# Block transposes and copies for every quad of an attention kernel, two placed tiles, output weights loaded one at a time, queries loaded by quad

## The chip, the cores and the metric

The kernel runs on one core of one Trainium2 chip. The metric is the device time in microseconds of one execution; the median of several runs counts. Engines are named as the profile names them: PE is TensorE, DVE is VectorE, ACT is ScalarE, POOL is GpSimd, SP is SyncE, which here only issues transfers.

## The reference, cut to what matters

Four conditional layers are added onto x (32 sequences of 32 rows, 512 wide). The first three are projections with weights picked by index; the fourth is attention over a paged cache, where nearly all of the time goes.

```python
B, S, HID, D, HQ, HK = 32, 32, 512, 128, 32, 8      # as drawn here; 16 pages of 32 keys
q = rope(rmsnorm(x @ Wq.T)); k = rope(rmsnorm(x @ Wk.T)); v = x @ Wv.T
k_all = concatenate([k_cache[block_table], k]); v_all = concatenate([v_cache[block_table], v])
scores = einsum('bqhd,bkhd->bhqk', q, k_all) * SCALE      # 512 cached keys + 32 new ones
scores = where(valid, scores, -1e30)
probs  = softmax(scores)
o      = einsum('bhqk,bkhd->bqhd', probs, v_all)
x      = x + o.reshape(b, s, HQ * D) @ Wo.T
```

Four query heads share one key head, so that one key head of one sequence is a product of 128 query rows (4 heads x 32 rows) with 544 keys.

## The kernel before, in words

**First part.** x goes through the three small layers tile by tile (8 tiles of 128 rows). Then twelve chunks of 512 columns are projected (`projected`, L296): eight of queries, two of keys, two of values. PE does four accumulating matmuls per tile and chunk; DVE, ACT and POOL normalize and rotate; DVE transposes blocks of 32x32 (L349), and SP stores the heads to HBM (L358), four stores of 64 KB per tile. The weights of the next chunk are loaded on ACT's queue. The output weights `wo` (8 MB) are loaded on SP's queue, four transfers of 512 KB at the start of each of the chunks 3 to 6 (L640). Four tiles of the last chunk are left for later (`FILLS`).

**Attention.** The work is 256 units (b, g), b the sequence and g the key head, and four units of one sequence make a quad. The order on PE, DVE, ACT, POOL and SP is the program's own order, written out by hand: a loop over steps n emits, for each step,

- on SP at g = 0: the keys of the next sequence, 16 pages of 128 KB, behind the new values (`vn`), new keys and queries. On POOL at g = 7: the values, 16 pages. Both live in two homes by turns (`homes[b % 2]`). All of SP's transfers share eight completion slots: one waits until the eighth before it has landed;
- `scores`: two score matmuls (L680, L681) into the only score buffer in PSUM, then one DVE instruction that scales, masks and takes the minimum (L687, `pr`, `low`);
- `exponentials`: ACT's exponential with the sum (L698), and a small copy of the 32 new keys' probabilities into `pq` (L701);
- the probabilities' transpose[...]. For the second quad of a sequence PE transposes four blocks of 128x128 (`flip`, L741) and ACT copies them out (L743). For the first quad DVE transposes blocks of 32x32 (`turn`, L714) and sixteen copies of 32 partitions set the blocks in place (`place`, L730 on ACT, L732 on DVE);
- `values`: four value matmuls (L763) of the unit seven steps back; at a quad's end four more with the new keys' values (L775), and `keep` on DVE (L786, L788, L791), which divides by the sum and transposes;
- `flip_new` once a quad: PE transposes `pq` (L750), ACT copies it out (L752);
- `share`: output matmuls (L808) of the tile of four sequences finished before, dealt over 32 steps. At the first of them the residual x is loaded into a buffer of its own (L807); behind the last, DVE adds (L817) and SP stores (L818).

The places around the change that a sentence can't give:

```python
            if 2 <= n < N + 2 and (n - 2) % QUAD == QUAD - 1:
                flip_new(units[n - 2][0], units[n - 2][1] // QUAD)   # behind values(n)
...
    SHARE = [1, 2] * 5 + [1] + [1, 1, 1, 0] * 5 + [1]
```

Of the kernel before, what the change touches and what calls it, by code (L numbers as in the profile page):

```python
# [19 lines left out]
P = 128  # L20
# [36 lines left out]
def cond_resid_kernel(  # L57
# [44 lines left out]
    pk = const.tile([1, B + B * NPP], I32, name="pk")  # L102
# [5 lines left out]
    nc.sync.dma_start(out=pk, in_=pick)  # L108
# [12 lines left out]
    key_f = const.tile([P, LT], F32, name="key_f")  # L121
# [6 lines left out]
    def constant_values():  # L128
        nc.gpsimd.memset(eps_t, EPS)
        nc.gpsimd.memset(half_pi, HALF_PI)  # L130

        nc.gpsimd.iota(
            key_f[:, :L],
            pattern=[[1, L]],
            base=0,
            channel_multiplier=0,
            allow_small_or_imprecise_dtypes=True,
        )
        nc.vector.memset(key_f[:, L:], -4.0e9)
        nc.vector.tensor_copy(len_f, ii[:, C_SEQ : C_SEQ + B])  # L140
# [18 lines left out]

    class Picked:  # L160
# [3 lines left out]
        def __init__(self, eng, src: bass.AP, at: int, dsts, shape: str):  # L164
            self.eng, self.src, self.at, self.dsts, self.shape = eng, src, at, dsts, shape
            self.rows = []
            for _ in range(AHEAD):
                self.name_next()

        def name_next(self):  # L170
            n = self.at + len(self.rows)
            self.rows.append(
                nc.values_load(
                    pk[0:1, n : n + 1],
                    engines=(self.eng.engine,),
                    min_val=0,
                    max_val=self.src.shape[0] - 1,
                    skip_runtime_bounds_check_because="rows are drawn from the array's own range",
                )
            )  # L180
# [9 lines left out]
    homes, kts, vts, vns, news = {}, {}, {}, {}, {}  # L190
# [4 lines left out]
    def load_keys(b: int):  # L195

        pool = homes[b % 2]
        kt = pool.tile([P, NPP + 1, HK * PSIZE], F32, tag="kt", name=f"kt_{b}")
        qt = pool.tile([P, HQ * S], F32, tag="qt", name=f"qt_{b}")
        kts[b], news[b] = kt, qt  # L200
# [3 lines left out]
    def see_keys(b: int):  # L204

        nc.vector.tensor_scalar(
            mask, key_f, len_f[:, b : b + 1], -1.0e30, ALU.is_ge, ALU.mult
        )

    def load_new_keys(b: int):  # L210
        nc.sync.dma_start(out=kts[b][:, NPP, :], in_=k_d[b])
        nc.sync.dma_start(out=news[b], in_=q_d[b])
# [414 lines left out]
    vnp = ctx.enter_context(tc.tile_pool(name="b_vn", bufs=3, side="right"))  # L627
# [3 lines left out]
    for c in range(1, NCH):  # L631
        if c + 1 < NCH:
            load_qkv(c + 1, nc.scalar)
        if c == 2:
            load_pages(0)
            load_values(0)
        if 3 <= c < 7:
            r = c - 3
            for k in range(D // S):
                nc.sync.dma_start(  # L640
                    out=wo[r * S : (r + 1) * S].rearrange("d (g k) o -> d g k o", g=HK)[:, :, k, :],
                    in_=w_o4[r, k],
                )
        if c == (HQ + HK) // REP:

            while ready:
                store_heads(*ready.pop(0))
            turn.close()
            turn_n.close()
            ps_p = ctx.enter_context(tc.tile_pool(name="b_p", bufs=1, space=PSUM, side="right"))  # L650
            load_new_keys(0)
            open_home(1)
            load_keys(1)
            load_new_keys(1)
            load_pages(1)
            load_values(1)
        for t in range(1 if c == 1 else 0, NT if c < NCH - 1 else NT - FILL):
            projected(c, t, 2)
            if c == NCH - 1 and t == 2:
                load_new_values(0)  # L660
                load_new_values(1)
# [6 lines left out]
    dens, news_p, prs, pos = {}, {}, {}, {}  # L668
# [5 lines left out]
    def scores(b: int, g: int):  # L674
        kt, qt = kts[b], news[b]
# [3 lines left out]
        q = qt[:, g * REP * S : (g + 1) * REP * S]  # L679
# [4 lines left out]
        pr = tp.tile([P, LT], F32, tag="pr", name=f"pr_{b}_{g}", bufs=4)  # L684
# [7 lines left out]
    def exponentials(b: int, g: int, pr, low):  # L692
        quad, u = quad_of(b, g), g % QUAD
        if u == 0:
            dens[quad] = tp.tile([P, QUAD], F32, tag="den", name=f"den_{b}_{g}", bufs=4)
            prs[quad] = {}
            news_p[quad] = tp.tile([P, QUAD, S], F32, tag="pq", name=f"pq_{b}_{g}")
# [3 lines left out]
        nc.scalar.copy(news_p[quad][:, u, :], pr[:, L:])  # L701
        prs[quad][u] = pr
# [3 lines left out]
    turned, placed = {}, {}  # L706

    def turn(b: int, us):
        if 0 in us:
            turned[b] = tp.tile(  # L710
                [P, P // S, QUAD, L // P, S], F32, tag="turned", name=f"turned_{b}", bufs=1
            )
        for u in us:
            nc.vector.transpose(  # L714
                turned[b][:, :, u, :, :].rearrange("p j c s -> p c j s"),
                prs[b, 0].pop(u)[:, :L].rearrange("p (c j s) -> p c j s", j=P // S, s=S),
            )

    def place(b: int, i: int, on_act: int):

        if i == 0:
            placed[b] = tp.tile(
                [P, QUAD, L // P, P], F32, tag="placed", name=f"placed_{b}", bufs=1
            )
        for j in range(P // S):
            dst = placed[b][j * S : (j + 1) * S, :, :, i * S : (i + 1) * S]
            src = turned[b][i * S : (i + 1) * S, j, :, :, :]
            dst, src = (a.rearrange("p u c s -> p (u c) s") for a in (dst, src))
            if j < on_act:
# [3 lines left out]

    pts = {}

    def flip(b: int, g: int):

        pr = prs[quad_of(b, g)].pop(g % QUAD)
        pp = ps_p.tile([P, L // P, P], F32, tag="p", name=f"p_ps_{b}_{g}")
        for c in range(L // P):  # L740
            nc.tensor.transpose(pp[:, c, :], pr[:, c * P : (c + 1) * P], ident)  # L741
        pts[b, g] = tp.tile([P, L // P, P], F32, tag="pt", name=f"pt_{b}_{g}")
        nc.scalar.copy(pts[b, g], pp)  # L743
# [3 lines left out]
    def flip_new(b: int, q: int):  # L747

        pnp = ps_p.tile([P, P], F32, tag="p", name=f"pn_ps_{b}_{q}")
        nc.tensor.transpose(pnp, news_p.pop((b, q)).rearrange("p u s -> p (u s)"), ident)  # L750
        pns[b, q] = tp.tile([P, P], F32, tag="pn", name=f"pn_{b}_{q}", bufs=3)
        nc.scalar.copy(pns[b, q], pnp)  # L752

    def values(b: int, g: int):
# [6 lines left out]
        pt = pts.pop((b, g)) if q else placed[b][:, u, :, :]  # L761
# [8 lines left out]
        if u == QUAD - 1:  # L770
            pn = pns.pop((b, q))

            for i in range(QUAD):
                r = slice(i * S, (i + 1) * S)
                nc.tensor.matmul(po[:, i, :P], pn[r, :], vn[r, q, :], start=False, stop=True)  # L775
            keep(b, q)
# [19 lines left out]
    pfs, x3s = {}, {}  # L796

    BLOCKS = list(range(HALF, HQ)) + list(range(HALF))

    def finish(t: int, ns):  # L800

        for n in ns:
            h = BLOCKS[n]
            if n == 0:
                pfs[t] = ps_p.tile([P, HID], F32, tag="f", name=f"f_ps_{t}")
                x3s[t] = tp.tile([P, HID], F32, tag="x3", name=f"x3_{t}", bufs=1)
# [5 lines left out]
                start=(n == 0),  # L812
                stop=(n == HQ - 1),
            )
            if n == HQ - 1:
# [3 lines left out]

    SHARE = [1, 2] * 5 + [1] + [1, 1, 1, 0] * 5 + [1]

    def share(n: int):
        t, i = divmod(n - 3 - BT * HK, BT * HK)
# [6 lines left out]
    LAG = 7  # L833

    ON_ACT = [[2, 2, 2, 4], [1, 1, 1, 3]]

    FILLS = {0: NT - 4, 1: NT - 3, 3: NT - 2, 5: NT - 1}
# [7 lines left out]
    with tc.manual_schedule(engines=order):  # L845
        for n in range(N + LAG):
            b, g = divmod(n, HK)
            at = B + (b + 1) * NPP
# [4 lines left out]
            if n < N:  # L853
                if g == 0 and 1 <= b < B - 1:
                    load_keys(b + 1)
                    keys = Picked(nc.sync, k_cache, at, page_keys(b + 1), K_SHAPE)
                    load_new_values(b + 1)
                    load_new_keys(b + 1)
                    keys.transfer()
                if g == 7 and 1 <= b < B - 1:  # L860
                    values_in = Picked(nc.gpsimd, v_pages, at, page_values(b + 1), V_SHAPE)
                    values_in.transfer()
                scored = scores(b, g)

            if 2 <= n < N + 2 and units[n - 2][1] >= QUAD:
                flip(*units[n - 2])
            if n < N:
# [4 lines left out]
            if n < N and g in (3, 4):  # L872
                turn(b, (0, 1) if g == 3 else (2, 3))
            if n >= LAG and (n - LAG) % HK < QUAD:
                bm, i = divmod(n - LAG, HK)
                place(bm, i, ON_ACT[bm + 1 >= BT][i])
            if n >= LAG:
                bv, i = divmod(n - LAG, HK)
                values(bv, (i + QUAD) % HK)
                if i == HK - 1:  # L880
                    placed.pop(bv), turned.pop(bv)
            if 2 <= n < N + 2 and (n - 2) % QUAD == QUAD - 1:
                flip_new(units[n - 2][0], units[n - 2][1] // QUAD)
            if n < N and g == HK - 1 and b < B - 1:
                see_keys(b + 1)
            share(n)
            if n >= N + 3:
                finish(NT - 1, range(3 * (n - N - 3), 3 * (n - N - 2)))
        assert not dens and not news_p and not pos and not pts and not pns
        finish(NT - 1, range(12, HQ))  # L890


# [74 lines left out]
```

## Time and profile before

| | us |
|---|---|
| median of 3 runs (1298.12 to 1298.87) | 1298.71 |
| the profiled execution's own time | 1300.91 |
| its span, first to last instruction | 1299.2 |
| PE busy | 1247.2 |
| DVE busy | 762.2 |
| ACT busy | 661.9 |
| POOL busy | 382.0 |

The profiled execution lies 2.2 us above the median; 1.7 us of its time are outside the span. In the page, a group's row gives line, engine, operation, output and input tiles, shapes and count, then busy time and mean length, then the engine's idle time just before, with what ended it. The chain follows the last instruction back to what released it, step by step. The granted clock is the share of full speed at which PE was allowed to run. The first part ends at some 447 us, where the loop over steps begins; the last score matmul is at 1254 us.

### The profile page before, as it was taken

What the parts mean: (1) busy time and instruction counts of PE and PEld (TensorE: products, weight loads), DVE (VectorE), ACT (ScalarE), POOL (GpSimd) and SP (SyncE); (2) the same over time, 40 slices, a digit from 0 to 9 for tenths busy, and PEclk for the clock granted to TensorE, in tenths of its full rate; (3) what the DMA queues carried; (4) which work ended last, traced back from release to release, by engine and by line L of the source; (5) the groups of instructions that cost most, each with busy time, mean ns of one, the idle gap of its engine ahead of it and who ended that gap; (6) DMA issues with size and microseconds to landing.
All of it is one profiled execution on the core that took longest, in us unless ns stands there. A gap on an engine that the chain in (4) does not pass through costs nothing.

```text
span 1299.2 us, 22028 instructions
## 1 busy us (share of the span) xinstructions
PE 1247.2 (96%) x5992; PEld 799.5 (62%) x5992; DVE 762.2 (59%) x1742; ACT 661.9 (51%) x1701; POOL 382.0 (29%) x619
## 2 busy tenths in 40 slices
PE   9999998899999988899999999999999999999998
PEld 5444443334444457767777777777777777777774
DVE  3233775666786046656666666666666665665660
ACT  1232554554455266755555556555655654665550
POOL 2311532223343202422332332233223322432310
PEclk9999999998899999999999999999999999999999
DMA  8985856666445836996888887988877997897710
GB/s 340 421 327 186 247 151 149 152 157 156 111 123 154 252 122 163 218 223 175 209 206 192 199 225 180 202 208 199 219 192 184 219 217 170 214 213 202 175 53 17
DMA packets 181964, 250.80 MB, mean 193 GB/s; under 512 B 26545, under 2 KB 145713, under 8 KB 176082
## 3 DMA queue, kind: packets, MB, share of 16 engines
q1 hardware_dynamic: 152738, 165.35, 47.0%
q0 software_dynamic: 25360, 69.37, 22.8%
q10 hardware_dynamic: 3744, 14.68, 3.2%
q8 instruction: 49, 0.80, 0.3%
q14 instruction: 73, 0.60, 0.2%
HBM read 219.94 MB, written 29.36 MB: 192 GB/s over the span
## 4 chain that ended last, share of the span: by engine, by line
PE 82%; ACT 10%; DMA 3%; DVE 3%; issue 2%; SPq 1%; POOL 0%; DVEq 0%; ACTq 0%
PE qkv L296 26%; PE f_ps L808 16%; PE o_ps L763 15%; PE s_ps L680 8%; PE s_ps L681 7%; ACT placed L730 4%; PE p_ps L741 4%; ACT pr L698 3%; PE adapt L484 2%; DMA wa<-in_w_adapt_dram 2%; DVE pr L687 1%; PE o_ps L775 1%; PE base L464 1%; ACT pq L701 1%; ACT pt L743 0%
## 5 line engine op out<-in xcount | busy, mean ns | idle before, releaser
L185 POOL DMA_DIRECT2D vt<-in_v_cache_dram x480 | 244.8, 510 | 553.1 <-PE o_ps L763 361.9
L296 PE MATMUL qkv<-wq,x3t 128*128 128x512 f32 x768 | 343.2, 608 | 14.5 <-DVE rs L334 14.5
L687 DVE CUSTOM_DVE_ANT_0 pr<-s_ps,mask 128x544 f32<-128x544 f32 x256 | 185.1, 723 | 275.2 <-PE s_ps L681 240.4
L698 ACT ACTIVATE pr<-pr,low 128x544 f32<-128x544 f32 x256 | 191.8, 749 | 167.4 <-DVE low L687 164.1
L296 PEld LDWEIGHTS qkv<-wq,x3t 128*128 128x128 f32 x768 | 148.8, 195 | 204.5 <-issue 204.3
L808 PE MATMUL f_ps<-wo,ot 128*128 128x512 f32 x512 | 257.6, 605 | 0.0
L340 POOL TENSOR_TENSOR ra<-ra,rs 128x512 f32<-128x512 f32 x80 | 101.5, 1269 | 253.3 <-DVE rs L334 194.8
L680 PE MATMUL s_ps<-kt,qt 128*128 128x288 f32 x512 | 170.4, 415 | 1.9 <-DVE low L687 1.9
L763 PE MATMUL o_ps<-vt,placed 128*128 128x128 f32 x1024 | 139.7, 280 | 20.3 <-ACT placed L730 20.3
L342 ACT ACTIVATE ra<-ra,rinv 128x128 f32<-128x128 f32 x320 | 102.2, 390 | 108.0 <-POOL ra L340 106.6
L743 ACT COPY pt<-p_ps 128x512 f32<-128x512 f32 x128 | 75.0, 586 | 159.9 <-PE p_ps L741 159.6
L763 PEld LDWEIGHTS o_ps<-vt,placed 128*128 128x128 f32 x1024 | 131.1, 194 | 36.9 <-ACT placed L730 32.1
L681 PE MATMUL s_ps<-kt,qt 128*128 128x256 f32 x512 | 153.0, 381 | 0.0
L680 PEld LDWEIGHTS s_ps<-kt,qt 128*128 128x128 f32 x512 | 92.7, 191 | 96.5 <-issue 79.4
L732 DVE COPY placed<-turned 32x512 f32<-32x512 f32 x308 | 132.2, 429 | 6.3
L763 PE MATMUL o_ps<-vt,pt 128*128 128x128 f32 x1024 | 135.1, 275 | 0.0
L763 PEld LDWEIGHTS o_ps<-vt,pt 128*128 128x128 f32 x1024 | 126.8, 192 | 1.6
L730 ACT COPY placed<-turned 32x512 f32<-32x512 f32 x204 | 125.5, 615 | 2.0
L681 PEld LDWEIGHTS s_ps<-kt,qt 128*128 128x128 f32 x512 | 97.8, 191 | 27.5 <-DMA vn<-v_d 0.3
L808 PEld LDWEIGHTS f_ps<-wo,ot 128*128 128x128 f32 x512 | 82.2, 190 | 37.2 <-issue 30.1
L318 DVE TENSOR_REDUCE ss<-sq 128x4 f32<-128x512 f32 x80 | 53.8, 673 | 65.5 <-ACT sq L316 65.3
L714 DVE STREAM_TRANSPOSE turned<-pr 128x512 f32<-128x512 f32 x128 | 83.2, 688 | 3.0 <-ACT placed L730 3.0
(95 smaller groups left out, 999.9 us busy)
## 6 DMA issues: line engine op xcount, KB each, us to landing
vt<-in_v_cache_dram POOLq DMA_DIRECT2D x512, 128.0 KB, 6.6
kt<-in_k_cache_dram SPq DMA_DIRECT2D x512, 128.0 KB, 7.1
wa<-in_w_adapt_dram SPq DMA_DIRECT2D x32, 1024.0 KB, 9.4
q_d<-st SPq DMA_DIRECT2D x256, 64.0 KB, 1.8
qt<-q_d SPq DMA_DIRECT2D x32, 512.0 KB, 5.7
wq<-in_w_qkv_dram ACTq DMA_DIRECT2D x10, 1024.0 KB, 5.1
wo<-in_w_o_dram SPq DMA_DIRECT2D x16, 512.0 KB, 8.7
k_d<-st SPq DMA_DIRECT2D x64, 64.0 KB, 1.8
```

The lines of the kernel that those rows point to most:

```text
L185: self.eng.dma_start(out=out, in_=row)
L296: nc.tensor.matmul(ps, x3[:, k, :], w[:, k, :], start=(k == 0), stop=(k == KC - 1),)
L340: nc.gpsimd.tensor_tensor(a, a, s, ALU.add)
L342: nc.scalar.activation(a[:, h, :], a[:, h, :], AF.Copy, scale=rinv[:, h : h + 1])
L680: nc.tensor.matmul(ps[:, first:L], q, kt4[:, :N_LOW, g, :], start=True, stop=True)
L681: nc.tensor.matmul(ps[:, L : first + LT], q, kt4[:, N_LOW:, g, :], start=True, stop=True)
L687: nc.vector.tensor_tensor_reduce(pr, ps[:, first : first + LT], mask, -SCALE, 3.0e38, ALU.add, ALU.min, low)
L698: nc.scalar.activation(pr, pr, AF.Exp, bias=low, scale=-1.0, accum_out=dens[quad][:, u : u + 1])
L730: nc.scalar.copy(dst, src)
L732: nc.vector.tensor_copy(dst, src)
L763: nc.tensor.matmul(po[:, u, :P], pt[:, c, :], vt[:, c, g * D : (g + 1) * D], start=(c == 0), stop=False,)
L808: nc.tensor.matmul(pfs[t], ots[t, h // HALF][:, h % HALF, :], wo[:, h, :], start=(n == 0), stop=(n == HQ - 1),)
```

## The change

- Both quads of each sequence go over DVE's block transposes and the placing copies; PE's `flip` and ACT's copy of it are gone. `place` now takes one quarter j of the keys of all four units per step: one DVE transpose of 128x512 into `turned` (two buffers), then four copies, of which `ON_ACT[j]` on ACT. `placed` has two buffers.
- `pr` holds a quad's four units in one tile (two buffers), and `pq` is filled by one copy of 128x128, inside `flip_new`, which is now emitted in the second step of the next quad, ahead of `place`, `share` and `values`.
- Values are eight steps behind the scores (`LAG` 8). `share` stands ahead of `values`, begins at step 36 and follows another pattern; heads are taken in their natural order.
- The residual x is loaded at the third last output matmul, into the buffer of `os`.
- Queries are loaded by quad (256 KB, three buffers); a sequence's new values at its own g = 0 (two buffers); cached values at g = 0 of their own sequence; the page numbers as small tables of 16.
- `wo` is loaded one transfer after every second tile of the chunks 3 to 6.
- The key numbers for the mask are 16-bit integers.

```diff
+    def load_table(b: int):
+        pages_of[b] = const.tile([1, NPP], I32, tag="pages", name=f"pages_{b}", bufs=4)
+        at = B + b * NPP
+        nc.sync.dma_start(out=pages_of[b], in_=pick[:, at : at + NPP])
...
-        nc.sync.dma_start(out=news[b], in_=q_d[b])
+    def load_queries(b: int, q: int):
+        qts[b, q] = qp.tile([P, HALF * S], F32, tag="qt", name=f"qt_{b}_{q}")
+        nc.sync.dma_start(
+            out=qts[b, q], in_=q_d[b][:, q * HALF * S : (q + 1) * HALF * S]
+        )
...
-        if 3 <= c < 7:
-            r = c - 3
-            for k in range(D // S):
-                nc.sync.dma_start(
...
         for t in range(1 if c == 1 else 0, NT if c < NCH - 1 else NT - FILL):
             projected(c, t, 2)
+            if 3 <= c < 3 + REP and t % 2 == 1:
+                r, k = c - 3, t // 2
+                nc.sync.dma_start(
...
-        pr = tp.tile([P, LT], F32, tag="pr", name=f"pr_{b}_{g}", bufs=4)
+        if u == 0:
+            prs[quad_of(b, g)] = tp.tile([P, QUAD, LT], F32, tag="pr", name=f"pr_{b}_{g}")
+        pr = prs[quad_of(b, g)][:, u, :]
...
-        nc.scalar.copy(news_p[quad][:, u, :], pr[:, L:])
...
+    def place(b: int, q: int, j: int, on_act: int):
+        if j == 0:
+            placed[b, q] = tp.tile([P, QUAD, L // P, P], F32, tag="placed", name=f"placed_{b}_{q}")
+        pr = prs[b, q][:, :, :L].rearrange("p u (c j s) -> p j u c s", j=P // S, s=S)[:, j]
+        part = tp.tile([P, QUAD, L // P, S], F32, tag="turned", name=f"turned_{b}_{q}_{j}")
+        nc.vector.transpose(part, pr)
+        for i in range(P // S):
+            dst = placed[b, q][j * S : (j + 1) * S, :, :, i * S : (i + 1) * S]
+            src = part[i * S : (i + 1) * S]
             dst, src = (a.rearrange("p u c s -> p (u c) s") for a in (dst, src))
-            if j < on_act:
+            if i < on_act:
                 nc.scalar.copy(dst, src)
             else:
                 nc.vector.tensor_copy(dst, src)
-    def flip(b: int, g: int):
-        pr = prs[quad_of(b, g)].pop(g % QUAD)
-        pp = ps_p.tile([P, L // P, P], F32, tag="p", name=f"p_ps_{b}_{g}")
-        for c in range(L // P):
-            nc.tensor.transpose(pp[:, c, :], pr[:, c * P : (c + 1) * P], ident)
...
     def flip_new(b: int, q: int):
         pnp = ps_p.tile([P, P], F32, tag="p", name=f"pn_ps_{b}_{q}")
-        nc.tensor.transpose(pnp, news_p.pop((b, q)).rearrange("p u s -> p (u s)"), ident)
-        pns[b, q] = tp.tile([P, P], F32, tag="pn", name=f"pn_{b}_{q}", bufs=3)
+        pq = tp.tile([P, QUAD, S], F32, tag="pq", name=f"pq_{b}_{q}", bufs=1)
+        nc.scalar.copy(pq, prs[b, q][:, :, L:])
+        nc.tensor.transpose(pnp, pq.rearrange("p u s -> p (u s)"), ident)
+        pns[b, q] = tp.tile([P, P], F32, tag="pn", name=f"pn_{b}_{q}")
         nc.scalar.copy(pns[b, q], pnp)
...
-                x3s[t] = tp.tile([P, HID], F32, tag="x3", name=f"x3_{t}", bufs=1)
+            if h == LATE:
+                x3s[t] = tp.tile([P, HID], F32, tag="os", name=f"x3_{t}", bufs=1)
                 nc.sync.dma_start(out=x3s[t], in_=x_d[t])
...
-    SHARE = [1, 2] * 5 + [1] + [1, 1, 1, 0] * 5 + [1]
+    LAG = 8
+    SHARE = [1, 2, 1, 2] * 2 + [1, 2, 1] + [1, 1, 0, 1] * 4 + [1, 1, 2]
+    BEGIN = BT * HK + LAG - QUAD
...
-    ON_ACT = [[2, 2, 2, 4], [1, 1, 1, 3]]
+    ON_ACT = [3, 3, 3, 2]
-    FILLS = {0: NT - 4, 1: NT - 3, 3: NT - 2, 5: NT - 1}
+    FILLS = {0: NT - 4, 2: NT - 3, 4: NT - 2, 6: NT - 1}
...
             if n < N:
+                if g == 0 and b >= 1:
+                    load_new_values(b)
                 if g == 0 and 1 <= b < B - 1:
                     load_keys(b + 1)
-                    keys = Picked(nc.sync, k_cache, at, page_keys(b + 1), K_SHAPE)
-                    load_new_values(b + 1)
+                    keys = Picked(nc.sync, k_cache, pages_of[b + 1], page_keys(b + 1), K_SHAPE)
                     load_new_keys(b + 1)
+                    load_queries(b + 1, 0)
                     keys.transfer()
-                if g == 7 and 1 <= b < B - 1:
...
+                    if b + 2 < B:
+                        load_table(b + 2)
+                if g == 0 and b >= 2:
+                    values_in = Picked(
+                        nc.gpsimd, v_pages, pages_of.pop(b), page_values(b), V_SHAPE
+                    )
                     values_in.transfer()
+                if g == QUAD and b < B - 1:
+                    load_queries(b + 1, 1)
                 scored = scores(b, g)
                 exponentials(*scored)
             if n in FILLS:
                 projected(NCH - 1, FILLS[n], 2)
...
+            if QUAD <= n < N + QUAD:
+                bq, i = divmod(n - QUAD, HK)
+                q, j = divmod(i, QUAD)
+                if j == 1:
+                    flip_new(bq, q)
+                place(bq, q, j, ON_ACT[j])
+            share(n)
             if n >= LAG:
...
+                values(*units[n - LAG])
...
-            if 2 <= n < N + 2 and (n - 2) % QUAD == QUAD - 1:
-                flip_new(units[n - 2][0], units[n - 2][1] // QUAD)
...
-            share(n)
```

## The prediction

> **What bounds the kernel now.** I read the page's head first, then the chain, the groups by shape, and the timeline of single steps.
>
> ```profile
> span 1299.2 us, 22028 instructions
> PE 1247.2 (96%) x5992; PEld 799.5 (62%) x5992; DVE 762.2 (59%) x1742; ACT 661.9 (51%) x1701; POOL 382.0 (29%) x619
> ...
> PE 82%; ACT 10%; DMA 3%; DVE 3%; issue 2%; SPq 1%; POOL 0%; DVEq 0%; ACTq 0%
> ```
>
> PE is 96% busy and holds 82% of the chain that ended last: a microsecond in which PE waits is lost, and PE work removed is gained. The groups by shape give the work concerned:
>
> ```profile
> L730 ACT COPY placed<-turned 32x512 f32<-32x512 f32 x204 | 125.5, 615 | 2.0
> L741 PE MATMUL p_ps<-ident,pr 128*128 128x128 f32 x512 | 77.8, 275 | 2.1 <-ACT pn L752 0.3
> L743 ACT COPY pt<-p_ps 128x512 f32<-128x512 f32 x128 | 75.0, 586 | 159.9 <-PE p_ps L741 159.6
> L750 PE MATMUL pn_ps<-ident,pq 128*128 128x128 f32 x64 | 17.7, 276 | 2.7 <-ACT pt L743 2.7
> ```
>
> The last row matters most: the 64 transposes of the new keys wait 2.7 us in all, because their input was copied steps earlier. One step's latency stands in the timeline (start, length):
>
> ```profile
> 657.90 0.59 PE L681 MATMUL s_ps<-kt,qt 128*128 128x256 f32 x2
> ...
> 658.54 0.72 DVE L687 CUSTOM_DVE_ANT_0 pr<-s_ps,mask 128x544 f32<-128x544 f32 x1 [1.39 <-PE s_ps L681]
> ...
> 659.31 0.75 ACT L698 ACTIVATE pr<-pr,low 128x544 f32<-128x544 f32 x1 [2.25 <-DVE low L687]
> ...
> 660.18 0.22 ACT L701 COPY pq<-pr 128x32 f32<-128x32 f32 x1
> ```
>
> PE's next work began at 658.34. ACT's first instruction behind the exponential starts 1.84 us later.
>
> [...] (PE idles 20.3 us before o_ps L763 for ACT's copies though score matmuls stand behind). [...] (stretch, PE busy, then PEclk third from the end):
>
> ```profile
> 484.00:485.00 1.00, 0.14 (x1) 0.14 (x2) 0.16 (x1) 0.96 (x3) 0.00 (x0) 1.00 0.87 227
> 485.00:486.00 1.00, 1.00 (x9) 1.00 (x10) 1.00 (x2) 0.89 (x3) 0.00 (x0) 1.00 0.14 43
> 505.00:507.00 2.00, 0.24 (x2) 0.00 (x0) 1.26 (x3) 1.97 (x4) 0.84 (x2) 1.00 1.05 210
> 507.00:508.00 1.00, 0.75 (x4) 0.76 (x5) 0.77 (x2) 0.97 (x3) 0.00 (x0) 0.68 1.08 235
> 508.00:509.00 1.00, 1.00 (x6) 1.00 (x6) 0.53 (x1) 0.28 (x2) 0.00 (x0) 0.50 1.11 234
> ```
>
> Three idle times of 2.00 us (until 484.86, 507.25, 531.29): two are followed by some 3.5 us at 0.5, one by none. The four of 3.63 us (until 226.2, 259.3, 293.5, 327.6) all are; the one of 1.50 (553.5) isn't. [...]
>
> **Part 1: transposes leave PE.** 128 groups of four at 0.44 us (598.10 minus 597.66 in the chain) are 56 us. PE's waits for `placed` change too, some 5 us per 32 steps: the work sums to 97 (per step scores 0.92, values 0.89, new keys 0.11, flips 0.22, new-key flip 0.03, output 0.86, each the distance between starts in the timeline), and 102 elapse (the output blocks in the chain recur from 557.34 to 659.39).
>
> **Part 2: DVE and ACT take them.** DVE: 128 more block transposes at 0.65 us, and 320 copies for 308. ACT: 704 copies for 204; 128 evacuations and 256 small copies go. Per quad (four steps) ACT needs four exponentials at 0.87 (with the accumulator read), 11 copies at 0.62, one pq (128x128; never seen: 0.22 as 128x32 here, 0.39 as L342's; I take 0.30) and pn 0.26: 10.9 us. DVE needs 4 x 0.80 + 4 x 0.65 + 5 x 0.43 + 1.57 for keep + 0.25 = 9.8. A quad had 12.1 (24.2 us per eight steps, 616.95 to 641.14), so neither engine is the bound by sum.
>
> **Part 3: the new wait.** `flip_new` moves to the second step of a quad, straight behind that step's scores on PE. Its pq copy stands on ACT behind the exponential of the *same* scores. PE in order holds values, output and the next scores behind it. Followed from the end of scores of the fourth step (t=0), three outputs per quad:
> - PE: output 0.86, values and new keys to 2.18, scores of the next quad's first step to 3.10.
> - DVE: minimum, transpose, two copies to 2.43; keep's product waits for PE, 2.6 to 3.3; transpose to 3.95; only then the next minimum, low ready at 4.7.
> - ACT: exponential 4.72 to 5.59, three copies to 7.46. PE ends the second step's scores at 5.77.
> - ACT: second exponential to 8.33, pq to 8.63; PE flips at 8.70. PE waited **2.9 us** (2.2 were ACT free).
> - Then values, scores, output, values, scores: 13.3; the mask (0.50 us, one quad in two, behind keep) makes it 13.5.
>
> So 13.5 for 12.1 with three outputs; the same walk gives 15.8 with six (before 13.4: SP's vn loads at 641.14 and 694.69, four quads) and 12.7 with none (before 12.0: 71.8 us from 471.89 to 543.73 for six quads).
>
> **Half clock.** Two of three at 2.0 us and four of four at 3.6 were throttled. I take 0.8 of the 2.9 us waits, each costing half of 3.5 us: 1.4 us per quad, an estimate between 0 and 2.9 (phases of 5.8 us, as from 259.3 to 265).
>
> **Part 4: x loaded late, in os's buffer.** The load is issued three outputs before the end (step 64+32t), on SP behind that step's vn, the register reads, 16 key pages and the table. SP's line before:
>
> ```profile
> 668.14 2.47 SPq L241 DMA_DIRECT2D vn<-v_d  x4
> 670.71 0.52 SPq L211 DMA_DIRECT2D kt<-k_d  x1
> 671.28 0.43 SPq L212 DMA_DIRECT2D qt<-q_d  x1
> 671.90 18.05 SPq L185 DMA_DIRECT2D kt<-in_k_cache_dram  x16
> ```
>
> From the end of step 63's scores: vn (two buffers now) waits for values of step 63, 2.2; vn 2.5; eight register reads at 0.27, 2.1; kt, qt 1.1; the keys 11 to 18 (four batches before took 15.8, 11.0, 15.0, 18.1); x lands 2.7 later at 22 to 29, say 25. DVE's add stands in step 65, before step 66's minimum, and with it every later one. It was due at 11; PE runs out of work at 14 (scores of step 67 need that minimum) and goes on at 26.4. That is 13 us (range 8 to 20), at six tiles; the seventh has no keys ahead. out's store must then land before keep writes os: 3 us, two steps off, hidden; if not, some 1 us.
>
> **Part 5: output weights singly.** The four 3.63 us gaps fall in the chunks with bursts of four, none in the later ones (119.78 us unbroken from 327.62). From 226.21 to 327.62 are 101.4 us for 192 passes at 0.429: 19.0 lost, with the first gap 22.7. Between two single loads there are eight 64 KB stores. I take -20, ends 0 and -23.
>
> **At nothing:** page tables (30 loads of 64 B on SP) and queries by quad (same bytes) lie beside PE work; without that cover 0.3 us of SP each. Keys reach the chip some 4 us later and need to be there 27 us later; only a faster kernel than I forecast would wait. Values (POOL, one step later) need 18 of 27. Integer mask: 32 x 0.50, plus or minus 0.2 each, 6 us.
>
> **Sum** against the profiled execution (1300.9 us, span 1299.2; the median is 2.2 lower). Per 32 steps, with the outputs dealt six, six, five and then three a quad: 15.8+15.8+15.0+5x13.5 = 114, with half clock 125.3, before 102.
> - First eight steps +3; next 24: 6 x 14.1 = 85 for 71.8, +13.
> - Steps 32 to 64: 125 for 100, +25.
> - Six tiles: 125.3 + 13 - 102, +36.3 each, +218.
> - Tail (last copies uncovered, 11 x 0.62 against four values) +5; front -20.
>
> 1300.9 + 244 = 1545, against the median **1543**.
>
> **The rivals.**
> - *No half clock* (2.9 us stay below the throttle as one 2.00 did): 1543 - 62 x 1.4 = **1456**.
> - *Longer throttle or later x*: 5.8 us phases add 0.8 x 1.15 x 62 = 57, 20 us waits 42: some **1595**.
> - *x lands in time* (keys in 11 us, as 620.84 to 631.85, and less beside them): minus 6 x 13, **1465**.
> - *Faster*: the flip's wait hides. PE then needs 89.8 per cycle (97 less the flips), which ACT's 10.9 in quads of three outputs and keep stretch to some 95.5: 0.8 us gained per quad, and 0.3 from the front. So a wait above 1.1 us per quad decides for slower whatever x does. Without it and with x in time, 6.5 x 7 + 3 + 20 are gained: **1230**. For it: the flips wait 2.7 us in all now. Against it: minimum and exponential alone take 1.84. That the transposes don't leave PE is excluded by the changed program's instruction order, which also shows the flip directly behind its step's scores.
>
> **How the numbers follow.** Forecast 0.62, no half clock 0.18, longer 0.10, x in time 0.05, faster 0.04, a tie 0.01. Both slower rivals and the unknown sizes set 1440 to 1620, leaving some 0.18 out. About 0.2% is what a measurement of this kernel tells from no change: faster 0.04, within 0.01, slower 0.95.
>
> **What would show it.** pn_ps should be waiting for ACT pq, some 180 us in 64 times; PEclk near 0.9 from step 8 on; DVE's add waiting for DMA x some 6 times; no gaps from 226 to 330; PE's busy share down to some 80 to 85%. If pn_ps waits less than 40 us in all, the core of this is wrong.

## The result and the profile after

The changed kernel takes 1599.1 us (median of 4 runs, 1590.67 to 1606.81), the kernel before 1298.41 (1295.04 to 1298.87). The ratio is 1.2321, 95% interval 1.224 to 1.2403: slower, with 1543 us forecast. The profiled execution took 1590.67 us, the lowest of the four.

The head of the page after, and its chain:

```profile
span 1589.0 us, 21379 instructions
PE 1279.9 (81%) x5480; PEld 789.2 (50%) x5480; DVE 846.8 (53%) x1882; ACT 867.0 (55%) x1881; POOL 380.2 (24%) x619
...
PE 29%; DVE 8%; ACT 7%; SPq 3%; DMA 3%; issue 2%; ACTq 0%; DVEq 0%
```

PE runs 512 instructions less and is nevertheless busy 33 us longer (1247.2 before): its clock was granted at 0.924, before at 0.987. It also stands still for 309 us, before for 52. DVE and ACT do more, as planned, but neither is near full: the loss lies in waiting. The groups by shape (busy time and mean length, then idle time before them) answer to those shown of the kernel before:

```profile
L733 ACT COPY placed<-turned 32x512 f32<-32x512 f32 x704 | 432.7, 615 | 13.2 <-DVE turned L727 4.2 <-ACT vs L318 0.8
...
L744 PE MATMUL pn_ps<-ident,pq 128*128 128x128 f32 x64 | 23.2, 362 | 155.3 <-ACT pq L743 152.1 <-issue 3.1
...
L743 ACT COPY pq<-pr 128x128 f32<-128x128 f32 x64 | 18.1, 282 | 0.0
...
L811 DVE TENSOR_TENSOR x<-x,f_ps 128x512 f32<-128x512 f32 x8 | 5.5, 688 | 122.8 <-DMA x<-x_d 100.0 <-PE f_ps L802 22.8
```

The 64 small transposes, which waited 2.7 us in all, now wait 155.3. The waits of PE (total us, times, longest) name two more places. The last row is the kernel before's row for the third of them:

```profile
PE pn_ps L744 <- ACT pq L743: 152.1, 63, 2.6
PE s_ps L696 <- DVE low L705: 85.2, 32, 13.5
PE qkv L308 <- DVE rs L346: 36.4, 10, 3.6
...
PE qkv L296 <- DVE rs L334: 14.5, 4, 3.6
```

**The first**, in the timeline of one quad (start, length):

```profile
780.06 0.59 PE L697 MATMUL s_ps<-kt,qt 128*128 128x256 f32 x2
...
780.70 0.72 DVE L705 CUSTOM_DVE_ANT_0 pr<-s_ps,mask 128x544 f32<-128x544 f32 x1 [0.20 <-PE s_ps L697]
...
782.14 0.75 ACT L714 ACTIVATE pr<-pr,low 128x544 f32<-128x544 f32 x1
...
782.89 0.28 ACT L743 COPY pq<-pr 128x128 f32<-128x128 f32 x1
...
783.23 0.33 PE L744 MATMUL pn_ps<-ident,pq 128*128 128x128 f32 x1 [2.57 <-ACT pq L743]
```

The copy's data were ready a step before, but it stands behind the exponential of the newest scores, and PE's transpose stands directly behind those scores. That exponential itself comes some 0.7 us late: its `low` was there at 781.42, but ACT was busy until 782.12 with three placing copies of the step before.

**The second** is the end of an output tile. First the transfers that SP issues (SPq), then DVE and PE:

```profile
730.93 2.62 SPq L253 DMA_DIRECT2D vn<-v_d  x4
736.54 0.34 SPq L217 DMA_DIRECT2D kt<-k_d  x1
736.94 0.42 SPq L222 DMA_DIRECT2D qt<-q_d  x1
737.58 13.61 SPq L192 DMA_DIRECT2D kt<-in_k_cache_dram  x16
751.30 0.29 SPq L165 DMA_DIRECT2D pages<-in_pick_dram  x1
751.68 0.34 SPq L801 DMA_DIRECT2D x<-x_d  x1
```

```profile
754.63 0.69 DVE L811 TENSOR_TENSOR x<-x,f_ps 128x512 f32<-128x512 f32 x1 [17.57 <-DMA x<-x_d]
...
756.02 1.33 PE L696 MATMUL s_ps<-kt,qt 128*128 128x288 f32 x2 [13.49 <-DVE low L705]
```

PE's row names DVE's `low`, but DVE itself was held by the load of x. **The third** is in the first part, PE alone:

```profile
253.72 8.80 PE L308 MATMUL qkv<-wq,x3t 128*128 128x512 f32 x16 [3.64 <-DVE rs L346]
266.15 9.88 PE L308 MATMUL qkv<-wq,x3t 128*128 128x512 f32 x16 [3.64 <-DVE rs L346]
279.67 9.95 PE L308 MATMUL qkv<-wq,x3t 128*128 128x512 f32 x16 [3.63 <-DVE rs L346]
292.39 8.71 PE L308 MATMUL qkv<-wq,x3t 128*128 128x512 f32 x16 [2.77 <-issue]
```

There are 13 such gaps up to 407.12, one at every second tile, where the kernel before had four of 3.63 us. (Ten of the 13 are in the row of waits above; the profile gives the other three as "issue".) The first score matmul starts at 498.2 us, before at 447.2. For this part a gain was forecast.

By place, the spans differ by 289.8 us: 53.1 until the new keys' load of step 8 (525.03, before 471.89), 39.6 from there to that of step 64 (736.54, before 643.81), and 197.1 behind it. The steps were timed on profiled runs; the medians differ by 11 us more.

### The profile page after: what moved, and what is told of

It reads as the page before. It is cut to its first block, busy times and chain, and to the rows that moved or that the text cites. A ratio compares the mean times of both kernels' runs of the same rounds, so it can differ in the third digit from the quotient of the medians.

```text
span 1589.0 us, 21379 instructions
## 1 busy us (share of the span) xinstructions
PE 1279.9 (81%) x5480; PEld 789.2 (50%) x5480; DVE 846.8 (53%) x1882; ACT 867.0 (55%) x1881; POOL 380.2 (24%) x619
## 4 chain that ended last, share of the span: by engine, by line
PE 29%; DVE 8%; ACT 7%; SPq 3%; DMA 3%; issue 2%; ACTq 0%; DVEq 0%
PE f_ps L802 10%; PE o_ps L757 9%; PE s_ps L696 4%; PE s_ps L697 4%; ACT pr L714 3%; ACT placed L733 3%; DVE pr L705 3%; DMA kt<-in_k_cache_dram 2%; DVE ot L786 1%; DVE os L783 1%; SPq L180 1%; PE o_ps L769 1%; DVE turned L727 1%; SPq L192 1%; PE pn_ps L744 1%
## 5 line engine op out<-in xcount | busy, mean ns | idle before, releaser
L733 ACT COPY placed<-turned 32x512 f32<-32x512 f32 x704 | 432.7, 615 | 13.2 <-DVE turned L727 4.2
L308 PE MATMUL qkv<-wq,x3t 128*128 128x512 f32 x768 | 364.0, 635 | 44.7 <-DVE rs L346 36.4
L757 PEld LDWEIGHTS o_ps<-vt,placed 128*128 128x128 f32 x2048 | 287.8, 205 | 112.1 <-issue 95.0
L757 PE MATMUL o_ps<-vt,placed 128*128 128x128 f32 x2048 | 289.7, 288 | 11.2 <-ACT placed L733 11.0
L802 PE MATMUL f_ps<-wo,ot 128*128 128x512 f32 x512 | 267.3, 628 | 3.5 <-DVE ot L786 3.5
L696 PE MATMUL s_ps<-kt,qt 128*128 128x288 f32 x512 | 191.5, 458 | 85.2 <-DVE low L705 85.2
L727 DVE STREAM_TRANSPOSE turned<-pr 128x512 f32<-128x512 f32 x256 | 180.9, 706 | 0.1
L354 ACT ACTIVATE ra<-ra,rinv 128x128 f32<-128x128 f32 x320 | 102.2, 390 | 124.1 <-POOL ra L352 122.9
L744 PE MATMUL pn_ps<-ident,pq 128*128 128x128 f32 x64 | 23.2, 362 | 155.3 <-ACT pq L743 152.1
L802 PEld LDWEIGHTS f_ps<-wo,ot 128*128 128x128 f32 x512 | 101.0, 204 | 52.0 <-issue 37.0
L328 ACT ACTIVATE sq<-qkv 128x512 f32<-128x512 f32 x80 | 46.8, 587 | 81.7 <-PE qkv L308 81.6
```

The lines of the kernel that those rows point to most:

```text
L308: nc.tensor.matmul(ps, x3[:, k, :], w[:, k, :], start=(k == 0), stop=(k == KC - 1),)
L354: nc.scalar.activation(a[:, h, :], a[:, h, :], AF.Copy, scale=rinv[:, h : h + 1])
L696: nc.tensor.matmul(ps[:, first:L], q, kt4[:, :N_LOW, g, :], start=True, stop=True)
L727: nc.vector.transpose(part, pr)
L733: nc.scalar.copy(dst, src)
L757: nc.tensor.matmul(po[:, u, :P], pt[:, c, :], vt[:, c, g * D : (g + 1) * D], start=(c == 0), stop=False,)
```

## The experiments

**1. The wait in front of the transpose.** Theory: it is made by the place of copy and transpose, and costs half-rate time besides. Rivals: the clock doesn't follow, or the wait moves on.

```diff
-                if j == 1:
-                    flip_new(bq, q)
                 place(bq, q, j, ON_ACT[j])
+                if j == 0:
+                    copy_new(bq, q)             # the pq copy, taken out of flip_new
             share(n)
             if n >= LAG:
                 values(*units[n - LAG])
+            if QUAD <= n < N + QUAD and j == 1:
+                flip_new(bq, q)
```

> The changed kernel, with the copy of the new keys' probabilities issued one step earlier on ACT (at the end of the quad's next step) and the transpose issued on PE behind the step's values instead of right behind its scores. Theory (the transpose waits for the copy, and each wait also costs half-rate matmuls behind it): the 152 us of PE idle in front of the transpose go, and 64 x 1.4 us of half rate with them, so 1599 - 240 = about 1360 us, and the granted clock rises above 0.96. Rival 1 (only the wait counts, the clock does not follow from it): 1599 - 152 = about 1447 us with the clock near 0.92. Rival 2 (the wait moves on to the next scores, since ACT is late there anyway): over 1560 us.

Measured: 1445.17 us (1441.46 to 1448.57), 154 less, and the clock 0.942. The total is that of rival 1, but not by its sum. In the profiled runs PE's idle time fell by 100 us (309.1 to 208.8) and its busy time by 49 (1279.9 to 1231.0): the clock follows, though not as far as the 0.96 expected. The wait did not go wholly, and a part of it moved on, as PE's wait for `low` rose from 85.2 us:

```profile
PE s_ps L696 <- DVE low L705: 99.0, 27, 15.8
...
PE pn_ps L749 <- ACT pq L743: 29.0, 32, 0.9
```

In half of the quads the copy, now the last of its step on ACT, was still late by 0.9 us. So a second form puts it first in that step:

```diff
+                if j == 0:
+                    copy_new(bq, q)
                 place(bq, q, j, ON_ACT[j])
-                if j == 0:
-                    copy_new(bq, q)
```

> The changed kernel, with the copy of the new keys' probabilities as the first ACT work of the quad's next step (ahead of that step's placing) and the transpose behind the values of the step after. The earlier form still left 29 us of wait in 32 quads. Theory: the whole of the wait in front of the transpose goes, 155 us, and of the busy time about 60 us (0.4 us for each us of wait, as the first form had it): about 1400 us. Rival (the 29 us were hidden behind other waits): 1445 us.

Measured: 1425.67 us (1422.28 to 1430.93), 173.4 below the changed kernel. No wait of `pn_ps` for `pq` is left. It gained 20 us on the first form where 45 were expected: waits for `placed` rose from 16.1 to 27.3 us, PE waited 8.4 us for keys (0.7 in the first form) and 3.2 for queries, and its busy time did not fall further (1237.5 us).

The counter-test puts the order of the changed kernel into the kernel before. The fourth copy is held back until the newest exponential has been issued, and the transpose, in the same step as before, moves from behind the values to directly behind the scores:

```diff
-        nc.scalar.copy(news_p[quad][:, u, :], pr[:, L:])
+        if u < QUAD - 1:
+            nc.scalar.copy(news_p[quad][:, u, :], pr[:, L:])
+        else:
+            last[quad] = pr
...
+        nc.scalar.copy(news_p[b, q][:, QUAD - 1, :], last.pop((b, q))[:, L:])  # in flip_new
...
+            if QUAD < n < N + 2 and n % QUAD == 1:      # behind exponentials(n)
+                flip_new(units[n - 2][0], units[n - 2][1] // QUAD)
...
-            if 2 <= n < N + 2 and (n - 2) % QUAD == QUAD - 1:      # behind values(n)
-                flip_new(units[n - 2][0], units[n - 2][1] // QUAD)
```

> The kernel before, with one edit: the last of a quad's four copies of the new keys' probabilities is made two steps later on ACT, behind that step's exponential, and the transpose follows at once, as in the changed kernel; nothing else moves. Theory (the wait is from the place of copy and transpose alone): 1.3 to 2.4 us of wait in each of 64 quads, 115 to 150 us, and about 0.4 us of half rate for each: 1460 to 1510 us. Rival (the wait needs the changed kernel's fuller ACT): under 1400 us.

Measured: 1473.7 us (1467.05 to 1479.19), against 1300.27: 173.4 us more, ratio 1.1323 (1.1292 to 1.1354). The group says where:

```profile
L754 PE MATMUL pn_ps<-ident,pq 128*128 128x128 f32 x64 | 21.6, 337 | 129.0 <-ACT pq L753 126.8 <-issue 2.1
```

PE's busy time rose by 64.4 us (1247.2 to 1311.6) with the same work. ACT was busy for 45% of the span only, so a fuller ACT isn't needed for the wait. Copy and transpose directly behind the newest work cost 173 us in one kernel, and taking them away gains 173 in the other. That the two totals agree so closely is chance: PE's busy time moves by 64.4 us in the one and by 42.4 in the other (1279.9 to 1237.5).

**2. The end of an output tile.** Theory: the load of x is late because it stands behind the keys. Rival: SP would then wait for the buffer. The edit issues it at the start of the step, in front of the key loads.

```diff
+                if g == 0 and b > BT and b % BT == 0:
+                    load_x3(b // BT - 2)        # x3 in os's buffer, as before the edit
                 if g == 0 and 1 <= b < B - 1:
                     load_keys(b + 1)
```

> The changed kernel with the load of the residual rows (x3) issued on SP at the start of the same step, ahead of the next sequence's key loads instead of behind them; its buffer and everything else stay. Theory (the load is late because it stands behind the key pages' issues): the wait of VectorE for it, 100 us in six times, and PE's stall behind it go, about 6 x 15 us = 90 us: about 1509 us. Rival (SP now waits at the load for the buffer, and the keys come late instead): 1580 to 1620 us.

Measured: 1565.85 us (1560.37 to 1575.96): 33 us gained, not 90, and keys weren't what came late. DVE's waits name a successor that neither theory nor rival had:

```profile
DVE os L783 <- DMA out_dram<-x: 45.2, 6, 8.7
```

and SP's timeline shows why:

```profile
732.44 0.52 SPq L796 DMA_DIRECT2D x<-x_d  x1
...
736.74 13.13 SPq L192 DMA_DIRECT2D kt<-in_k_cache_dram  x16
...
750.36 0.36 SPq L815 DMA_DIRECT2D out_dram<-x  x1
```

The load now is early, but the *store* of the result still stands behind the 16 key pages, and holds the buffer that `keep` wants for `os`; PE in turn waits 56.0 us for the outputs that `keep` makes (3.5 in the changed kernel). With a buffer of its own for x neither matters; the 2 KB come from the queries.

```diff
-    qp = ctx.enter_context(tc.tile_pool(name="b_q", bufs=3, side="right"))
+    qp = ctx.enter_context(tc.tile_pool(name="b_q", bufs=2, side="right"))
...
-    LATE = HQ - 3
+    LATE = 0
...
-                x3s[t] = tp.tile([P, HID], F32, tag="os", name=f"x3_{t}", bufs=1)
+                x3s[t] = tp.tile([P, HID], F32, tag="x3", name=f"x3_{t}", bufs=1)
...
                 if g == 0 and b >= 1:
                     load_new_values(b)
+                    load_queries(b, 1)          # and load_queries(b + 1, 0) at g == QUAD
```

> The changed kernel with the residual rows in a buffer of their own, loaded when the first of a tile's 32 output matmuls is issued; the room is taken from the queries (two buffers instead of three, each quad's queries loaded as the other quad begins). Theory (both the late load and the late store of the result, which stand behind the key pages on SP, hold the shared buffer): the 100 us of VectorE's wait for the load go and nothing takes their place, with some half-rate time: about 1495 us. Rival (the loss at a tile's end is not the buffer's: PE or ACT is short there): over 1550 us.

Measured: 1519.1 us (1516.88 to 1520.91), 80 us gained. DVE waits for no transfer of x any more, and PE's waits for `low` fall from 85.2 to 10.1 us. The expectation was 24 us too low, as it took the whole 100 us of DVE's wait, of which PE only felt what was beyond its own stock of work.

**3. The first part.** Theory: how the output weights' loads are written in changes the planned order of DVE's instructions (this part is ordered by a planner). Rival: transfers or SP's queue hold it up. First the four bursts put back, all else as changed:

```diff
+        if 3 <= c < 7:                          # at a chunk's head
+            r = c - 3
+            for k in range(D // S):
+                nc.sync.dma_start(              # wo
...
-            if 3 <= c < 3 + REP and t % 2 == 1:
-                r, k = c - 3, t // 2
-                nc.sync.dma_start(
```

> The changed kernel with the output weights loaded as in the kernel before: four bursts of four at the heads of chunks 3 to 6, on SP's queue. Theory (the way in which the loads are written in sets the planned order of VectorE, and with it how often PE runs out of accumulators): the 13 gaps of about 3 us become the 4 of the kernel before, and 45 to 55 us go: about 1548 us. Rival (the steps taken in the prediction: bursts hold up the queue and cost 20 us against single loads): about 1619 us. Rival 2 (the front is long for another reason): 1599 us.

Measured: 1550.87 us (1548.36 to 1553.84), 48 us gained; the gaps are the four of before, at 225.16, 258.02, 291.06 and 325.10. Then the sixteen single loads at the changed kernel's own places, on another queue:

```diff
-                nc.sync.dma_start(      # wo, one transfer after every second tile
+                nc.gpsimd.dma_start(
```

> The changed kernel with the same sixteen single loads of the output weights at the same places of the program, on the GpSimd queue instead of SP's; the bytes moved and the tiles at which they are issued stay, only VectorE's planned order differs (no square sum stands ahead of an older tile's rotation). Theory (order): none of the 13 gaps is left, 13 x about 5.5 us = 70 us go: about 1528 us. Rival (the loads disturb the front through the DMA engines): 1585 to 1610 us, gaps as they were.

Measured: 1524.04 us (1521.57 to 1529.57), 75 us gained. PE's timeline of this kernel from 215 us on is one row:

```profile
215.65 204.45 PE L308 MATMUL qkv<-wq,x3t 128*128 128x512 f32 x476
```

Same bytes, same tiles, no gap; but the queue changed together with DVE's order. What makes a gap is seen in the changed kernel's timeline ahead of the one that ends at 304.74:

```profile
298.40 0.69 DVE L330 TENSOR_REDUCE ss<-sq 128x4 f32<-128x512 f32 x1 [1.08 <-ACT sq L328]
...
301.83 0.69 DVE L330 TENSOR_REDUCE ss<-sq 128x4 f32<-128x512 f32 x1 [2.75 <-ACT sq L328]
...
302.44 0.70 DVE L361 STREAM_TRANSPOSE st<-ra 128x512 f32<-128x512 f32 x1
...
303.24 0.69 DVE L336 TENSOR_TENSOR ra<-qkv,cw 128x512 f32<-128x512 f32 x1
...
303.85 0.42 DVE L340 TENSOR_TENSOR rs<-qkv,sw 128x256 f32<-128x256 f32 x1
...
304.18 0.42 DVE L346 TENSOR_TENSOR rs<-qkv,sw 128x256 f32<-128x256 f32 x1
...
304.74 8.80 PE L308 MATMUL qkv<-wq,x3t 128*128 128x512 f32 x16 [3.64 <-DVE rs L346]
```

DVE sums the squares of the two newest tiles first, waiting for ACT to square PE's result of each, and only then runs `ra` and `rs` of an older tile, which free that tile's accumulator in PSUM. There are six accumulators (four and two), taken in turn. If a tile's `rs` stands behind the sum of the fifth tile after it, then PE has finished that fifth tile and has no accumulator for the sixth until `rs` has run. In DVE's instruction order this is so at 13 tiles of the changed kernel, at 4 of the kernel before and of the one with bursts, and at none with the loads on GpSimd's queue: the numbers of gaps seen. In the changed kernel each gap ends some 0.5 us after such an `rs` starts, at the sixth tile after it. Transfers aren't what holds DVE: between 190 and 447 us its waits in that kernel are for ACT's `sq` (68.9 us), `ra` (36.0) and `rms` (7.7), and no transfer is among them. The same in the kernel before, first the single loads, then its own bursts on GpSimd's queue:

```diff
+            if 3 <= c < 3 + REP and t % 2 == 1:     # single loads; the bursts removed
+                r, k = c - 3, t // 2
+                nc.sync.dma_start(
```

```diff
             for k in range(D // S):                 # bursts, in the other kernel
-                nc.sync.dma_start(
+                nc.gpsimd.dma_start(
```

> The kernel before with the output weights loaded singly as in the changed kernel, the only edit. Theory (order: 13 gaps for 4): 1299 + 9 x 5.7 = about 1350 us. Rival (the step of the prediction: single loads free the queue): about 1279 us.

> The kernel before with its four bursts of output weights on the GpSimd queue. Theory (order): its four gaps of 3.63 us go, each with its half-rate matmuls: 1299 - 4 x 5.7 = about 1276 us. Rival (the gaps are not of the order): 1299 us.

Measured: single loads 1348.52 us (1346.86 to 1349.83; 1.0397, 1.0371 to 1.0422), 13 gaps; GpSimd's queue 1274.44 (1273.02 to 1275.31; 0.9821, 0.9796 to 0.9846), none. Both within 2 us of the expectation. One run was to part order and queue: the single loads on SP's queue, at chunks 7 to 10.

```diff
-            if 3 <= c < 3 + REP and t % 2 == 1:
-                r, k = c - 3, t // 2
+            if 7 <= c < 7 + REP and t % 2 == 1:
+                r, k = c - 7, t // 2
```

> The changed kernel with the same sixteen single loads of the output weights, still on SP's queue, but at the tiles of chunks 7 to 10 instead of 3 to 6. In VectorE's planned order the square sum of the fifth tile after stands ahead of a tile's rotation at 2 tiles, where it does at 13 in the changed kernel. Theory (the order makes the gaps): 2 gaps of about 3 us, so 1524 + 2 x 5.7 = about 1535 us. Rival (the loads on SP's queue hold up the stores of the heads, wherever they stand): 1585 to 1610 us.

Measured: 1565.05 us, spread over 1551.22 to 1577.43 (1563.18 without the longest of the four). It falls between both and parts them only in half. Six gaps came in the first part, not 13, but not the 2 counted either: the two tiles counted are those of the last two gaps (until 386.69 and 400.17), and the count doesn't explain the four before them, from 341.98 on. Besides, PE waited another 12.97 us for the first scores, because SP was late:

```profile
444.57 0.57 SPq L671 DMA_DIRECT2D wo<-in_w_o_dram  x1
450.44 3.71 SPq L370 DMA_DIRECT2D k_d<-st  x8
454.19 0.44 SPq L217 DMA_DIRECT2D kt<-k_d  x1
```

So with the loads on SP's queue at these places the first scores came late too: the next store was issued 5.9 us behind the load of 444.57. That the load itself held it was not shown: SP's waits between 190 and 460 us name DVE's `st` (73.8 us), `wq` (32.5) and `v_d` (27.7), not `wo`. For the 13 gaps of the changed kernel the order suffices. Why the planner orders DVE so when a load is written between two tiles was not settled, nor was the order held fixed with the loads left where they are.

**4. All three together**, for what the change is worth without them. Its edits are those of the second form of the transpose, of x's own buffer and of the GpSimd queue:

```diff
+                if j == 0:
+                    copy_new(bq, q)             # flip_new behind values at j == 1
...
+    LATE = 0                                    # x3 under its own tag
...
+                nc.gpsimd.dma_start(            # wo, singly
```

> The changed kernel with three edits at once: the output weights' single loads on the GpSimd queue, the copy of the new keys' probabilities as the first ACT work of the quad's next step with its transpose behind the values of the step after, and the residual rows in a buffer of their own. Theory (these three account for the loss, and what the change removes is then seen): 1599 - 75 - 180 - 100 = about 1245 us. Rival (the new placement of all quads leaves ACT or VectorE short in every step, so that their copies become the bound once PE no longer waits): over 1320 us.

Measured: 1258.99 us (1254.31 to 1263.03), ratio to the kernel before 0.9705 (0.9666 to 0.9743): faster than both kernels. The rest of the change is still in it, DVE's and ACT's added work above all, so that this work isn't the loss. The three edits alone gain 173.4, 80.0 and 75.1 us, sum 328.5; together they gain 340. The head of its page:

```profile
span 1256.2 us, 21397 instructions
PE 1188.3 (95%) x5480; PEld 753.7 (60%) x5480; DVE 838.9 (67%) x1882; ACT 862.7 (69%) x1881; POOL 391.7 (31%) x635
```

PE is busy 46 us less than in the kernel before with GpSimd's queue (1234.6), which is near the 56 that the prediction gave the transposes; 30 come back as idle time (67.9 against 38.2). Of these, 11.5 us are waits for transposed outputs, 6.3 longer waits for placed tiles (26.6 against 20.3), and the rest waits of several kinds in front of the scores. The change proper thus gains some 15 us, 1.2% (1258.99 against 1274.44, runs of one chip). The intervals of the two against the kernel before, 0.9666 to 0.9743 and 0.9796 to 0.9846, lie apart. A last version aimed at those waits:

```diff
-            share(n)
+            first_output = (n - BEGIN) % (BT * HK) == 0
+            if not first_output:
+                share(n)                        # else behind values(n)
...
-                place(bq, q, j, ON_ACT[j])
+                place(bq, q, j, ON_ACT[j] if n >= BEGIN else (3, 3, 2, 1)[j])
```

> The version with three edits, and two more: a tile's first output matmuls stand behind the step's values instead of ahead of them, and before the outputs begin two of a quad's eleven ACT copies go to VectorE. Theory: the 11.5 us of wait for the transposed outputs and most of the 16 us of wait for placed tiles in the first steps go: about 1242 us. Rival (VectorE, with more copies, becomes late in the first steps): 1259 us or more.

Measured: 1256.7 us (1250.25 to 1261.16), 0.9682 (0.9656 to 0.9707). The wait for outputs is gone; that for placed tiles is not (29.7 us). The interval overlaps that of the version above, so no gain is shown.

## Why the prediction was right, and where it wasn't

- **Part 3, the new wait: right in place, somewhat too long.** 2.9 us per quad were forecast and 180 us in 64 times; 152.1 us in 63 times came, 2.4 us each, near the 2.2 worked out for a free ACT. `pq` took 0.282 us, for 0.30 assumed.
- **Half clock: right in kind, too dear.** 1.4 us per quad was taken, 0.8 of the waits throttled. Cut into stretches of 1 us from 750 to 1250, the counter-test shows 69 below three quarters of the clock, in 20 phases, each behind one of the 32 transposes there: 0.63 of the waits and 3.45 us a phase, 1.1 us per quad. Its busy time says 1.0 (64.4 / 64). In the changed kernel it was less still: 12 of the 30 transposes in the same stretch have such a phase behind them, 37 stretches in all, which is 0.6 us per quad, and the two forms with copy and transpose moved gave back 0.7 to 0.8 (42.4 and 48.9 us of busy time in 64 quads).
- **Part 4, the late x: right.** 13 us of stall at six tiles make 78; PE stood 13.49 us in the case shown, and a buffer of its own gains 80. "Out's store must land, hidden" holds in the changed kernel; it became the next wait once the load was early.
- **The steps.** From step 8 to 64 38 us were forecast, 39.6 came. A cycle of 32 steps takes 135.9 us (730.93 to 866.84), the four after it 132.8 to 136.9, forecast 138.3; with x in its own buffer it takes 122.9 from step 64 on, where 125.3 were worked out without the stall. What follows step 64 costs 197 us, forecast 223 with the tail.
- **Part 5 failed: -20 forecast for the first part, +51 came at the first score matmul.** The four gaps were put down to the bursts' transfers because they lay in the chunks with bursts, and "Between two single loads there are eight 64 KB stores" was the reason for their going. The rows of the kernel before already named DVE's `rs` as releaser, not a transfer. It was an order of instructions that the planner chose, and the change moved that from 4 tiles to 13. "No gaps from 226 to 330" was the sign that would show this step wrong; it did.
- **The sum.** 244 us were forecast on the profiled execution and 290 came. Up to step 8 (-17 forecast, 53.1 came) 70 us were missed, between step 8 and 64 1.6; 26 too many stood behind step 64: 70 + 1.6 - 26 = 46. Against the medians, 1543 for 1599.1, the forecast was 3.5% low. That it came so near is in part luck, since the 26 offset a part of the 70. The rival at 1595 lies nearer, but neither of its grounds came: phases behind the transposes' waits were 3.1 to 3.5 us, not 5.8, and PE's stalls 13.5 us at most, not 20.
- **The rival "faster"** needed the wait hidden, x in time and the front no worse; with all three put right it is 1259 us, where 1230 was worked out. The first part gave its share: GpSimd's queue alone takes 23 us off the kernel before, where 20 were taken. The attention did not: six of its seven cycles take 97.3 to 99.0 us, one 104.8, where 95.5 were worked out (before 101.9).

The signs named ahead otherwise came: `pn_ps` waiting for `pq`, DVE waiting for x six times, PE at 81%, the clock near 0.9.

## What to carry to other kernels

Data that were ready long ago can still reach an engine late, if their copy stands behind newer work (152.1 us of PE's waits in the changed kernel, none in the second form of experiment 1): place the copy ahead of the newest work of the copying engine, and the reader a step later. A small load or store behind sixteen page loads came late both ways here (DVE waited 100.0 us for the load of x and, once that was early, 45.2 for the store), so give it its own buffer, which gained 80 us, or its own queue, which was not tried for x, and look for the next holder when one wait is removed. In a part that a planner orders, adding or moving a transfer can reorder compute engines (single loads in place of bursts: 13 gaps for 4, 1348.52 us for 1300.27): compare the order of the instructions that free PSUM before crediting the transfer itself.

## What the runs showed of the hardware

Between 750 and 1250 us of the counter-test PE waited 63.6 us in front of 32 transposes, 1.99 us each in the mean, and half rate (a granted clock of 0.50) followed behind 20 of them, with 3.45 us a phase; in the same stretch of the kernel before, without these waits, the clock was 1.00 throughout. Length alone doesn't decide: of 30 waits of 1.89 to 2.57 us in the changed kernel only 12 did it, and of two of 2.57 us the one until 783.23 was followed by 0.50, the one until 846.52 by 1.00. Over the whole counter-test, waits of 126.8 us came with 64.4 us more of PE's busy time for the same work.
